# Neighbourhood attention on Trainium2: turned softmax weights in the expansion's PSUM banks, a third row of taps in two halves, and a new order for the second pass

## The chip, the cores and the metric

The kernel runs on one core of a Trainium2 chip. The metric is the device time of one launch in microseconds. Engines are named as in the profile: PE is the matrix engine (TensorE), PEld its weight loads, DVE is VectorE, ACT is ScalarE, POOL is GpSimd, SP is SyncE (it issues the loads and stores). SBUF is the on-chip memory with 128 partitions, PSUM the accumulators of the matrix engine, in banks of 512 float32 per partition.

## The reference

The input `x` is (4, 192, 128, 128) in float32: four images of 192 channels. Two layers follow each other.

Layer 0 is a channel-attention block: a 1x1 convolution to four times 192 channels, a depthwise 3x3 convolution, attention over the 24 channels of each of 8 heads, a gate from pooled values, and a 1x1 projection.

Layer 1 is what the change touches:

```python
pe = depthwise_conv3x3(x, pos_w)
x  = x + pe + pos_b
qkv = einsum('oc,bchw->bohw', qkv_w, x)            # 576 x 192
for i, dil in enumerate((1, 2, 3)):                # 64 channels each, 2 heads of 32
    k, v = 9 reflected neighbours at distance dil of every pixel
    attn = softmax(q . k / sqrt(32))               # over the 9 taps
    out_i = sum over the taps of attn * v
out = einsum('oc,bchw->bohw', proj_w, concat(out_i))
```

So each pixel of each image has 3 dilations x 2 heads x 9 taps of scores.

## The kernel before

The launch has three stages: the first pass (projection and depthwise convolution of layer 0, 0 to about 800 us), the channel attention (to about 1435 us), and the second pass, which applies layer 0's result and computes all of layer 1 (to the end). Only the second pass is changed.

*Tiling.* The second pass works in 64 blocks n. A block is 4 rows of 128 pixels (512 pixels) of a pair of images; blocks 0 to 31 are the first pair. The rows that the neighbours need are kept in rings in SBUF: `hboth` and `hring` for layer 1's input, `kring` and `vring` for keys and values of the three dilations g.

*What a block does*, in the order of its data:
- `loads` (L1089) bring x and v; `h_product` (L1102) makes three tiles of 128 x 512 (two of channels 0 to 127, one for each image, and a third with channels 128 to 191 of both images), and `h_evict` writes them into the rings.
- The position convolution of the first two tiles (`plan_conv`, L1229): `centre` on ACT (L1147) starts a sum in a query bank, `tap` (L1157) adds five taps on DVE, each reading the sum that the one before it wrote; three more taps are multiplied on ACT (`moved`) and added by accumulating transfers that POOL issues. Blocks 0 and 1 do all 8 taps on DVE.
- The third tile's nine taps are multiplied on ACT (`side`, L1192) into three rows of taps, two of these rows are added by accumulating transfers (`side_rows`, L1205), and POOL adds what is left (`side_sum`, L1213).
- `kv_product` (L1269) and `kv_evict` (L1289) fill the key and value rings; `query` and `query_rest` make the queries in PSUM; `prod` (L1346) multiplies on DVE a query with three taps of keys, 128 x 1536 elements; `pick_sums` (L1358) sums the products over the channels into one bank of scores `sc`.
- The softmax is a chain with one step at a time: scores copied by ACT, turned to pixels by PE (`by_pixel`, `st`), maximum and difference on DVE, exponential on ACT, sum on DVE, `divide` on POOL, and then the weights are split into three bf16 parts (`part0`, `rest`, `part1`, `part2`, on ACT and POOL).
- `turn` (L1451) turns the parts back with the rows as partitions, with matmuls of 128 x 128, in three groups i of four, each in a query bank `across`; `turned` (L1456) copies each group by ACT into `e_sb`.
- For each g and each row of taps ty: `expand` (L1495) spreads the weights of three taps over the channels, into the three banks of `ex`; `term` (L1502) multiplies them on DVE with the values, 128 x 1536 elements. The first two rows of taps (ty 0 and 1) are three matmuls on 32 rows each, in different 32-row strips of PE. In the third row, taps 6 and 7 are strips and tap 8 takes rows 0 to 63, because it has no strip of its own.
- `term_sum` (L1513) adds the three terms of a g: the second term is added to the first by an accumulating transfer that POOL issues (where `sent` is true: g = 0 and 1, and all g in the last three blocks) or by POOL; the third by POOL; and POOL then adds the three taps that are left side by side, in two sums of 512.
- `out_product` (L1527) projects, `out_evict` copies by ACT, `store` writes.

*PSUM.* The second pass has four pools: `pc` with two banks (h, k/v and output products), `ex` with one buffer of three banks, `q` with two (queries, the convolution's sums, and `across`), `sc` with one (scores and their turn).

*What sets the order.* Blocks overlap: while block n's weights are expanded, later blocks' products run. The instructions of each engine run in a fixed order, which a planner makes when the program is built. `Schedule` (L37) takes operations with an engine, a cost in microseconds, a rank, what they come after, and for PE the shape of the tile. It plays them engine by engine: of those that are ready it takes the lowest rank, where an operation whose PE shape differs from the last one's has `change_rank` added. It knows a delay of 0.2 between engines and none on the same engine, and 0.1 for a change of shape on PE. The rank is the block number plus an offset from a table, `PLACES` (L344), by `at(name, n, k)` = n + first + step * k. `hold(pool, bufs, first, last)` states that an operation takes a buffer and which operation gives it back, so that buffers limit the overlap. The order that comes out is what the program issues; at run time engines wait for each other by semaphores.

The functions of the second pass that the diff touches are these:

Of the kernel before, what the change touches and what calls it, by code (L numbers as in the profile page):

```python
# [8 lines left out]
BF16 = mybir.dt.bfloat16  # L9
# [10 lines left out]
G = 64  # L20
# [16 lines left out]
class Schedule:  # L37
# [10 lines left out]
    def add(self, engine, rank, cost, run, after=(), shape=None, latency=LATENCY):  # L48
        op = dict(engine=engine, rank=rank, cost=cost, run=run, shape=shape, latency=latency, seq=len(self.ops))
        op.update(after=list(after), first=[], users=[], issued=[])  # L50
        self.ops.append(op)
        return op
# [5 lines left out]
    def order(self):  # L58
# [28 lines left out]
        while events:  # L87
# [5 lines left out]
            for engine, ops in ready.items():  # L93
# [12 lines left out]
                for o in op["users"]:  # L106
                    release(o, end + op["latency"] * (o["engine"] != engine))
# [165 lines left out]
def rows3(t):  # L273
# [11 lines left out]
SUMMED, MOVED, TAP = (0, 1, 2, 7, 5), (3, 8, 6), 0.66  # L285
SLOTS = (0, 2, 4, 6, 1, 3, 5, 7)
# [58 lines left out]
    "loads": (8.8674, 0.08159),  # L345
    "h_product0": (-0.4546, 0.00000),
    "h_evict0": (4.2664, 0.11610),
    "h_product1": (-0.7453, 0.04958),
    "h_evict1": (-5.3389, 0.00000),
    "h_product2": (-0.5800, 0.00000),  # L350
    "h_evict2": (-1.5869, 0.00000),
    "centre": (0.6280, 0.26277),
    "tap": (2.4456, 0.00000),
    "moved": (25.2953, 0.22118),
    "moved_sum0": (8.0617, 0.20067),
    "moved_sum1": (25.2721, 0.04199),
    "side1": (16.4111, 0.19306),
    "side0": (16.3876, 0.02578),
    "side_rows0": (29.3597, 0.01803),
    "side2": (17.3819, 0.22411),  # L360
    "side_rows2": (11.5098, 0.04241),
    "side_sum1": (0.6333, 0.00000),
    "side_sum2": (9.6130, 0.00000),
    "kv0": (1.7001, 0.00000),
    "kvev0": (8.1270, 0.00000),
    "kv1": (2.9139, 0.00000),
    "kvev1": (9.1880, 0.00000),
    "kv2": (2.6117, 0.05333),
    "kvev2": (8.2682, 0.00000),
    "query0": (3.3163, 0.09055),  # L370
    "prod0": (8.3389, 0.00000),
    "query01": (24.1242, 0.00000),
    "term_sent": (10.6067, 0.00000),
    "query1": (3.4334, 0.00000),
    "prod1": (8.6064, 0.00000),
    "query2": (3.6386, 0.11339),
    "prod2": (8.6417, 0.08735),
    "pick0": (-12.0847, 0.00000),
    "pick1": (3.8649, 0.00000),
    "evicted_scores": (-5.2134, 0.00000),  # L380
    "by_pixel": (-11.8436, 0.07637),
    "top": (10.7097, 0.17234),
    "below": (12.3311, 0.00000),
    "exponential": (-3.5826, 0.00000),
    "total": (1.6598, 0.00000),
    "divide": (9.8505, 0.00000),
    "part0": (18.8851, 0.00000),
    "rest": (11.6606, 0.30882),
    "part1": (12.6889, 0.00000),
    "part2": (11.0247, 0.00000),  # L390
# [4 lines left out]
    "term_sum": (13.3772, 0.03133),  # L395
    "out0": (6.5430, 0.07136),
    "outev0": (-1.0619, 0.05980),
    "store0": (8.6802, 0.00000),
    "out1": (6.6681, 3.24309),
    "outev1": (-0.7072, 0.00000),  # L400
    "store1": (0.7313, 0.00000),
# [645 lines left out]
def second_pass(tc, x, w2, xv_p, mix1, mix2, biases, v_dram, v2_dram, out):  # L1047
# [4 lines left out]
    with ExitStack() as ctx:  # L1052
# [12 lines left out]
            (0.1, 3515.2787),  # L1065
# [55 lines left out]
        def plan_h(n):  # L1121
# [5 lines left out]
            for m in range(3):  # L1127
                us, shape = (0.86, FULL) if m < 2 else (0.87, COLS)
# [28 lines left out]
        def tap(n, im, t, last):  # L1157
# [6 lines left out]
            for at, length, o in runs(n, t // 3 - 1, RING, False):  # L1164
# [3 lines left out]
                    posw[:, 0, t : t + 1],  # L1168
                    acc[:, o : o + length],
# [201 lines left out]
        def plan_scores(n, y):  # L1371
            prods, used, picks = [], [], []
            first = [add("PE", at(f"query{g}", n), 0.87, (query, n, g), [y[2]], COLS) for g in range(NG)]
            both = add("PE", at("query01", n), 0.9, (query_rest, n, (0, 1)), first[:2] + y[3], QUARTERS)
# [10 lines left out]
            for row in range(7):  # L1385
                of = prods[4 * row // 3 : min(4 * row + 3, NG * NT - 1) // 3 + 1]
                op = add("PE", at(f"pick{row % 2 * (row < 6)}", n, row // 2), 0.86, (pick_sums, n, row), of, QUADS)
# [63 lines left out]
        def turn(n, i):  # L1451
            across = tile_of("q", ("across", n, i), (128, 4, W))
            for k in range(4):
                mm(across[:, k, :], parts[n % len(parts)][:, 4 * i + k], unit, start=True, stop=True)  # L1454
# [294 lines left out]
```

## Time and profile before

| What | Value |
|---|---|
| median of 3 runs | 4158.29 us (4155.67 to 4160.15) |
| the profiled execution's own time | 4148.03 us |
| its span | 4146.1 us |
| mean granted PE clock | 0.982 |
| busy, share of the span: PE, DVE, ACT, POOL | 97%, 90%, 69%, 75% |
| matmuls | 29088 |

How to read the profile: "busy" is time in which an engine has an instruction in work. Rows of a timeline give the start, the length, the engine, the line of the kernel, the operation, the tile written and the tiles read, the size, and how many instructions the row stands for; what stands in brackets is idle time of the engine before it and which instruction ended it. The length of a row of matmuls reaches to the end of its last result; the next group can start before that, since matmuls overlap, so the distance between the starts of two rows is the better measure of what a group takes. In the page's second part each digit is the busy share of one fortieth of the span, in tenths.

### The profile page before, as it was taken

The page shows a single profiled execution, that of the slowest core. Times are in us where ns is not written, and L with a number is a line of the kernel's source. Part 1 is how long each engine was busy: PE and PEld are TensorE (multiplying, and loading weights), DVE is VectorE, ACT ScalarE, POOL GpSimd, SP SyncE. Part 2 cuts the span into 40 slices and gives each one's busy share as a digit, 9 for nine tenths or more (in the row PEclk, how much of TensorE's full clock was granted, in tenths as well). Part 3 has the DMA queues.
Part 4 walks back from the last instruction along what each step waited for, and adds up shares of the span by engine and source line. Part 5 has one row for each costly group of instructions (what it writes and reads, how often), then busy time and mean ns, then how long its engine had stood idle before and what let it go on. Part 6 is the DMA issues. An engine that isn't in the chain of part 4 may idle for free.

```text
span 4146.1 us, 78135 instructions
## 1 busy us (share of the span) xinstructions
PE 4009.8 (97%) x29088; PEld 1578.6 (38%) x29088; DVE 3737.0 (90%) x4660; ACT 2857.5 (69%) x5337; POOL 3117.8 (75%) x2992
## 2 busy tenths in 40 slices
PE   8999999999999889999999999999999999999996
PEld 3333333356665523333333333333333333333321
DVE  6999999877676569999999999999999999999985
ACT  7999999844454477677676776767677776767741
POOL 6888888745455327888888888888888888888876
PEclk9999999999999999999999999999999999999996
DMA  8888888788778477878788787878878787878734
GB/s 252 267 266 257 270 267 262 227 220 209 199 194 209 124 165 168 185 168 186 169 177 175 171 184 169 181 165 181 174 174 180 170 185 167 186 170 177 154 76 94
DMA packets 404159, 785.08 MB, mean 189 GB/s; under 512 B 48008, under 2 KB 216772, under 8 KB 403780
## 3 DMA queue, kind: packets, MB, share of 16 engines
q0 software_dynamic: 73552, 315.47, 40.2%
q1 hardware_dynamic: 330228, 464.62, 37.5%
q8 instruction: 230, 3.77, 0.4%
q14 instruction: 149, 1.22, 0.1%
HBM read 278.09 MB, written 201.33 MB: 116 GB/s over the span
## 4 chain that ended last, share of the span: by engine, by line
PE 58%; DVE 3%; DMA 2%; issue 1%; POOL 1%; ACT 1%; SPq 0%; POOLq 0%; DVEq 0%; ACTq 0%
PE ph L1110 12%; PE sc L1363 10%; PE pkv L1276 8%; PE ex L1500 5%; PE po L1538 5%; PE pkv L1279 4%; PE q L1333 4%; PE po L1534 4%; PE st L1417 2%; PE q L1344 1%; DVE term L1508 1%; PE q L1340 1%; DVE prod L1352 1%; PE across L1454 1%; DMA side<-side 1%
## 5 line engine op out<-in xcount | busy, mean ns | idle before, releaser
L1352 DVE TENSOR_TENSOR prod<-q,kring 128x1536 f32<-128x1536 f32 (+1 forms) x600 | 997.6, 1685 | 46.0 <-PE sc L1363 32.5
L1508 DVE TENSOR_TENSOR term<-ex,vring 128x1536 f32<-128x1536 f32 (+1 forms) x600 | 1006.7, 1681 | 34.4 <-PE ex L1500 27.7
L1520 POOL TENSOR_TENSOR term<-term,term 128x1536 f32<-128x1536 f32 x253 | 899.4, 3555 | 57.0 <-DMA term<-term 40.9
L592 POOL TENSOR_TENSOR v_True<-v_True,side 128x512 f32<-128x512 f32 (+1 forms) x512 | 643.5, 1268 | 137.8 <-ACT side L581 111.1
L569 DVE SCALAR_TENSOR_TENSOR pa<-vboth,dwv,pa 128x1024 f32<-128x1024 f32 (+1 forms) x448 | 574.2, 1282 | 35.7 <-ACT pa L562 12.2
L1363 PE MATMUL sc<-prod,pick 128*32 128x512 f32 x3456 | 473.1, 603 | 3.1 <-DVE prod L1352 3.1
L1165 DVE SCALAR_TENSOR_TENSOR pa<-hboth,posw,pa 128x512 f32<-128x512 f32 (+1 forms) x524 | 393.0, 750 | 45.8 <-ACT hboth L1114 14.3
L1197 ACT ACTIVATE side<-hring,posw 128x512 f32<-128x512 f32 (+1 forms) x512 | 343.9, 714 | 95.6 <-DMA side<-side 95.5
L1276 PE MATMUL pkv<-y,wkv 128*128 128x512 f32 x768 | 375.4, 610 | 3.4 <-ACT kring L1289 1.4
L515 PE MATMUL pu<-xt,wx 128*128 128x512 f32 x768 | 358.4, 610 | 17.7 <-ACT vboth L551 10.3
L1110 PE MATMUL ph<-lent,mix 128*64 128x512 f32 (+1 forms) x1024 | 368.1, 596 | 4.7 <-DMA mix<-mixed 2.9
L581 ACT ACTIVATE side<-ring,dwv 128x512 f32<-128x512 f32 (+1 forms) x512 | 347.4, 723 | 25.2 <-POOL v_True L592 21.2
L809 DVE BATCH_NORM_STATS2 stats<-conv 128x6 f32<-128x128 f32 x1536 | 303.6, 273 | 61.0 <-ACT conv L807 60.1
L1289 ACT COPY vring<-pkv 64x512 f32<-64x512 f32 x384 | 223.5, 582 | 170.8 <-PE pkv L1279 158.1
L807 ACT COPY conv<-pc 128x512 f32<-128x512 f32 x384 | 228.0, 615 | 157.9 <-PE pc L798 150.1
L1500 PE MATMUL ex<-e_sb,spread 32*128 32x512 bf16 (+1 forms) x1728 | 289.7, 390 | 29.6 <-DVE term L1508 29.6
L798 PE MATMUL pc<-u,band 32*32 32x508 f32 (+1 forms) x6144 | 309.0, 626 | 8.9 <-DMA u<-qk_dram 4.1
L189 POOL COPY band<-few 32x720 f32<-32x720 f32 x180 | 141.6, 787 | 195.6 <-PE pc L798 177.4
L1525 POOL TENSOR_TENSOR acc<-acc,term 128x512 f32<-128x512 f32 x192 | 271.0, 1411 | 8.1
L1522 POOL TENSOR_TENSOR acc<-term 128x512 f32<-128x512 f32 x192 | 265.7, 1384 | 6.7 <-PE po L1534 1.8
L1500 PEld LDWEIGHTS <-spread 32*128 32x128 bf16 (+1 forms) x1728 | 75.1, 91 | 495.4 <-issue 449.4
L1289 ACT COPY kring<-pkv 64x512 f32<-64x512 f32 x384 | 223.2, 581 | 56.2 <-PE pkv L1279 49.1
(189 smaller groups left out, 7075.5 us busy)
## 6 DMA issues: line engine op xcount, KB each, us to landing
term<-term POOLq DMA_DIRECT2D x131, 768.0 KB, 6.5
qk_dram<-us SPq DMA_DIRECT2D x192, 512.0 KB
side<-side POOLq DMA_DIRECT2D x124, 768.0 KB, 8.9
u<-qk_dram SPq DMA_DIRECT2D x512, 128.0 KB
moved<-moved POOLq DMA_DIRECT2D x120, 512.0 KB, 6.0
xt<-in_x SPq DMA_DIRECT2D x64, 512.0 KB
v_dram<-v_False SPq DMA_DIRECT2D x64, 512.0 KB
lent<-in_x SPq DMA_DIRECT2D x128, 256.0 KB
```

What stands on the lines that cost most here:

```text
L515: mm(pu, wx[:, mt * 128 : (mt + 1) * 128], tiles["xt", n][:, im, :], start=True, stop=False)
L569: nc.vector.scalar_tensor_tensor(by_row(to[:, o : o + length]), by_row(vboth[:, at : at + length, :, t % 3 : t % 3 + W]), dwv[:, 0, t : t ...
L592: nc.gpsimd.tensor_add(v[:, rows, :], v[:, rows, :], z[:, rows, :])
L1110: mm(to, w[:, cols], tiles["xv", n, j, im], start=j == 0, stop=j == 2)
L1165: nc.vector.scalar_tensor_tensor(to[:, o : o + length], hboth[:, at : at + length, im, t % 3 : t % 3 + W], posw[:, 0, t : t + 1], acc[:, o ...
L1276: mm(rows3(tile_of("pc", key)), w, tiles["y", n, im], start=True, stop=False)
L1289: nc.scalar.copy(rows[HALVES[im ^ ((kind, g) == ("k", 1))], :, pad : pad + W], rows3(tiles["pkv", n, pair, im])[HALVES[e]])
L1352: nc.vector.tensor_mul(to[:, :, px].rearrange("p t (r w) -> p t r w", w=W), q.unsqueeze(1).to_broadcast([128, 3, *q.shape[1:]]), three,)
L1363: mm(sc[quad * 32 : (quad + 1) * 32, :], pick[:, QR - 4 * row : QR - 4 * row + 32], tiles["prod", n, k // NT, k % NT // 3][:, k % 3, :], s ...
L1500: mm(rows3(ex[:, t % 3, :]), spread[rows, t, :], e_sb[rows], start=True, stop=True)
L1508: nc.vector.tensor_mul(by_row3(to), by_row3(ex), three)
L1520: add_to(first, first, tiles.pop(("term", n, g, k + 1)))
```

## The change

Five things change, all in the second pass.

1. `turn` is one operation of 12 matmuls that writes the three banks of the `ex` pool, and `turned` is one ACT copy of 128 x 1536 elements to bf16. The query banks no longer hold `across`.
2. In `expand`, the third row of taps is done in the order 6, 8, 7, all three as matmuls on 64 rows: taps 6 and 7 on the one half of the rows (`HALVES[1]`), tap 8 on the other. The planner is told the shape ROWS (64 rows) for it.
3. The planner's `add` gets `own`: a delay between an operation and its user on the same engine, 0.13 for the taps. All offsets in `PLACES` are new, so is `change_rank`, and some costs (strips, third row, picks, a query, one h product).
4. In blocks 0 and 1 (`EARLY`) the third tile's position convolution is done as that of the other tiles: a centre on ACT in a query bank and 8 taps on DVE, in place of the nine `side` multiplications, two transfers and two POOL sums.
5. `sent` is true for g = 1 only in odd blocks (before: in all), and nowhere in the last block, n = 63. In the last block the second term is added to the first by DVE, in other cases that aren't sent by POOL.

```diff
-    def add(self, engine, rank, cost, run, after=(), shape=None, latency=LATENCY):
-        op = dict(engine=engine, rank=rank, cost=cost, run=run, shape=shape, latency=latency, seq=len(self.ops))
+    def add(self, engine, rank, cost, run, after=(), shape=None, latency=LATENCY, own=0.0):
+        op = dict(engine=engine, rank=rank, cost=cost, run=run, shape=shape, latency=latency, own=own, seq=len(self.ops))
...
-                    release(o, end + op["latency"] * (o["engine"] != engine))
+                    release(o, end + (op["latency"] if o["engine"] != engine else op["own"]))
...
+EARLY = 2
...
-    "turn": (4.4383, 0.12832),
-    "turned": (9.3688, 0.02210),
-    "expand": (-0.3709, 0.00000),
-    "term": (10.1902, 0.04882),
+    "turn": (-18.1522, 0.07377),
+    "turned": (5.9216, 0.14501),
+    "expand": (-18.0291, 0.00000),
+    "term": (4.9938, 0.00000),
...
-            (0.1, 3515.2787),
+            (0.1, 3164.4328),
...
+        def early_centre(n):
+            at = n * RB % RING
+            nc.scalar.activation(
+                rows3(tile_of("q", ("early", n))),
+                hring[2][:, at : at + RB, 1 : W + 1],
+                AF.Identity,
+                bias=posb[:, 2:3],
+                scale=posw[:, 2, 4:5],
+            )
+
+        def early_tap(n, t, last):
+            acc = to = rows3(tiles["early", n])
+            if last:
+                to = rows3(tile_of("y2", ("y", n, 2)))
+            for at, length, o in runs(n, t // 3 - 1, RING, False):
+                nc.vector.scalar_tensor_tensor(
+                    to[:, o : o + length],
+                    hring[2][:, at : at + length, t % 3 : t % 3 + W],
+                    posw[:, 2, t : t + 1],
+                    acc[:, o : o + length],
+                    ALU.mult,
+                    ALU.add,
+                )
...
-                    prev = add("DVE", at("tap", n, len(summed) * im + j), TAP, (tap, n, im, t, j == len(summed) - 1), [prev])
+                    prev = add("DVE", at("tap", n, len(summed) * im + j), TAP, (tap, n, im, t, j == len(summed) - 1), [prev], own=0.13)
...
+            if n < EARLY:
+                prev = first = add("ACT", at("early_centre", n), 0.65, (early_centre, n), latency=0.3)
+                read("h", 2, n, 0, first)
+                for j, t in enumerate(AROUND):
+                    prev = add("DVE", at("early_tap", n), TAP, (early_tap, n, t, j == 7), [prev], own=0.13)
+                    read("h", 2, n, t // 3 - 1, prev)
+                hold("q", first, prev)
+                return [prev, two, both, [both, prev]]
...
-        def turn(n, i):
-            across = tile_of("q", ("across", n, i), (128, 4, W))
-            for k in range(4):
-                mm(across[:, k, :], parts[n % len(parts)][:, 4 * i + k], unit, start=True, stop=True)
-
-        def turned(n, i):
-            if i == 0:
-                tile_of("e_sb", ("e_sb", n), (128, nh, W), BF16)
-            nc.scalar.copy(tiles["e_sb", n][:, 4 * i : 4 * i + 4, :], tiles.pop(("across", n, i)))
+        def turn(n):
+            across = tile_of("ex", ("across", n), (128, 3, PX)).rearrange("p b (q w) -> p (b q) w", w=W)
+            for k in range(nh):
+                mm(across[:, k, :], parts[n % len(parts)][:, k], unit, start=True, stop=True)
+
+        def turned(n):
+            e_sb = tile_of("e_sb", ("e_sb", n), (128, nh, W), BF16)
+            across = tiles.pop(("across", n))
+            nc.scalar.copy(e_sb.rearrange("p q w -> p (q w)"), across.rearrange("p b w -> p (b w)"))
...
-            out = []
-            for i in range(nh // 4):
-                a = add("PE", at("turn", n, i), 0.3, (turn, n, i), [p2, *out[-1:]], FULL)
-                out.append(add("ACT", at("turned", n, i), 0.58, (turned, n, i), [a, *out[-1:]]))
-                hold("q", a, out[-1])
+            a = then("PE", 0.66, turn, FULL)
+            out = then("ACT", 1.5, turned)
+            hold("ex", a, out)
...
-            for t in range(3 * ty, 3 * ty + 3):
-                rows = slice(0, G) if t == 8 else slice(SLOTS[t] // 2 * STRIP, (SLOTS[t] // 2 + 1) * STRIP)
+            for t in (6, 8, 7) if ty == 2 else range(3 * ty, 3 * ty + 3):
+                strip = SLOTS[t] // 2 * STRIP if t < 8 else 0
+                rows = HALVES[t < 8] if ty == 2 else slice(strip, strip + STRIP)
                 mm(rows3(ex[:, t % 3, :]), spread[rows, t, :], e_sb[rows], start=True, stop=True)
...
-            return ty == 1 and (g < 2 or n >= 2 * NB - 3)
+            return ty == 1 and n < 2 * NB - 1 and (g == 0 or g == 1 and n % 2 or n >= 2 * NB - 3)
...
+                if n == 2 * NB - 1 and k == 0:
+                    add_to = nc.vector.tensor_add
...
-                    ex = add("PE", at("expand", n, k), 0.36 if ty == 2 else 0.25, (expand, n, g, ty), w, STRIPS)
+                    ex = add("PE", at("expand", n, k), 0.43 if ty == 2 else 0.22, (expand, n, g, ty), w, ROWS if ty == 2 else STRIPS)
...
-                            prev = [add("POOL", at("term_sum", n, 4 * g + ty - 1), 3.5, (term_sum, n, g, ty - 1), after)]
+                            engine = "DVE" if n == 2 * NB - 1 and ty == 1 else "POOL"
+                            prev = [add(engine, at("term_sum", n, 4 * g + ty - 1), 3.5, (term_sum, n, g, ty - 1), after)]
```

More of the change, by code (lines that the diff above doesn't have):

```diff
@@ L344 @@
 PLACES = {
[L345 to L388, printed above, removed]
@@ L389 @@
-    "part1": (12.6889, 0.00000),
-    "part2": (11.0247, 0.00000),
-    "turn": (4.4383, 0.12832),
-    "turned": (9.3688, 0.02210),
-    "expand": (-0.3709, 0.00000),
-    "term": (10.1902, 0.04882),
[L395 to L401, printed above, removed]
+    "loads": (0.0099, 0.00000),
+    "h_product0": (-1.1442, 0.03236),
@@ new lines @@
+    "h_evict0": (0.9413, 0.00000),
+    "h_product1": (-0.5417, 0.00000),
+    "h_evict1": (46.0411, 0.00000),
+    "h_product2": (-0.4262, 0.00000),
+    "h_evict2": (-4.6711, 0.09271),
+    "centre": (0.4459, 0.61203),
+    "tap": (0.3422, 0.20258),
+    "moved": (17.0039, 0.14130),
+    "moved_sum0": (1.7081, 0.00000),
+    "moved_sum1": (6.3516, 0.14847),
+    "side1": (-4.7424, 0.01609),
+    "side0": (37.6996, 0.00000),
+    "side_rows0": (5.9045, 0.00000),
+    "side2": (38.3470, 0.27045),
@@ new lines @@
+    "side_rows2": (46.3059, 0.07396),
+    "side_sum1": (34.1352, 0.05190),
+    "side_sum2": (6.6114, 0.00000),
+    "kv0": (2.0359, 0.00000),
+    "kvev0": (4.4411, 0.00000),
+    "kv1": (2.6905, 0.12859),
+    "kvev1": (34.5720, 0.00000),
+    "kv2": (2.8325, 0.02873),
+    "kvev2": (3.1563, 0.00000),
+    "query0": (3.0813, 0.00000),
+    "prod0": (5.9337, 0.00000),
+    "early_centre": (0.8993, 0.00324),
+    "early_tap": (1.4758, 0.00000),
+    "query01": (-36.0721, 0.00000),
+    "term_sent": (-17.9540, 0.18186),
@@ new lines @@
+    "query1": (3.1570, 0.00000),
+    "prod1": (6.2578, 0.00000),
+    "query2": (3.5739, 0.00000),
+    "prod2": (6.7424, 0.00000),
+    "pick0": (-12.7266, 0.06397),
+    "pick1": (4.3024, 0.00000),
+    "evicted_scores": (3.6965, 0.16177),
+    "by_pixel": (-11.9922, 0.00000),
+    "top": (-19.9741, 0.00000),
+    "below": (1.1300, 0.00000),
+    "exponential": (2.8400, 0.11643),
+    "total": (5.4525, 0.00000),
+    "divide": (-10.5681, 0.12415),
+    "part0": (19.3124, 0.00000),
+    "rest": (-5.2533, 0.03124),
@@ L402 @@
+    "part1": (-2.3849, 0.02248),
+    "part2": (5.2677, 0.00000),
+    "turn": (-18.1522, 0.07377),
+    "turned": (5.9216, 0.14501),
+    "expand": (-18.0291, 0.00000),
+    "term": (4.9938, 0.00000),
+    "term_sum": (26.0187, 0.01071),
+    "out0": (6.3347, 0.11390),
+    "outev0": (0.0341, 0.00000),
+    "store0": (25.0600, 0.04627),
+    "out1": (6.6039, 0.21737),
+    "outev1": (1.0223, 0.00000),
+    "store1": (3.5346, 0.12892),
 }
@@ L1127, in plan_h @@
             for m in range(3):
-                us, shape = (0.86, FULL) if m < 2 else (0.87, COLS)
+                us, shape = (0.86, FULL) if m < 2 else (0.86, COLS)
                 ops = [add("PE", at(f"h_product{m}", n, j), us, (h_product, n, m, j), shape=shape) for j in range(3)]
@@ L1373, in plan_scores @@
             first = [add("PE", at(f"query{g}", n), 0.87, (query, n, g), [y[2]], COLS) for g in range(NG)]
-            both = add("PE", at("query01", n), 0.9, (query_rest, n, (0, 1)), first[:2] + y[3], QUARTERS)
+            both = add("PE", at("query01", n), 0.86, (query_rest, n, (0, 1)), first[:2] + y[3], QUARTERS)
             last = add("PE", at("query2", n, 1), 0.86, (query_rest, n, (2,)), first[2:] + y[3], FULL)
@@ L1386, in plan_scores @@
                 of = prods[4 * row // 3 : min(4 * row + 3, NG * NT - 1) // 3 + 1]
-                op = add("PE", at(f"pick{row % 2 * (row < 6)}", n, row // 2), 0.86, (pick_sums, n, row), of, QUADS)
+                op = add("PE", at(f"pick{row % 2 * (row < 6)}", n, row // 2), 0.83, (pick_sums, n, row), of, QUADS)
                 op["after"] += picks[-1:]
@@ L1485, in plan_softmax @@
             stage.schedule.hold("e", len(es), lo, [p2])
-            out = []
-            for i in range(nh // 4):
-                a = add("PE", at("turn", n, i), 0.3, (turn, n, i), [p2, *out[-1:]], FULL)
-                out.append(add("ACT", at("turned", n, i), 0.58, (turned, n, i), [a, *out[-1:]]))
-                hold("q", a, out[-1])
+            a = then("PE", 0.66, turn, FULL)
+            out = then("ACT", 1.5, turned)
+            hold("ex", a, out)
             stage.schedule.hold("parts", len(parts), p0, [a])
-            return out
+            return [out]
         def expand(n, g, ty):
```

## The prediction, made before the changed kernel was run

> **What bounds the kernel now.** I read the page first (engine sums, slices, chain of waits), then a window of the second pass, then single engines in order of time.
>
> ```profile
> span 4146.1 us, 78135 instructions
> ...
> PE 4009.8 (97%) x29088; PEld 1578.6 (38%) x29088; DVE 3737.0 (90%) x4660; ACT 2857.5 (69%) x5337; POOL 3117.8 (75%) x2992
> ...
> PE   8999999999999889999999999999999999999996
> ...
> PE 58%; DVE 3%; DMA 2%; issue 1%; POOL 1%; ACT 1%; SPq 0%; POOLq 0%; DVEq 0%; ACTq 0%
> ```
>
> PE is busy in every slice and carries 58% of the chain that ended last. The stretch that the change touches (from about 1435 us, 64 blocks):
>
> ```profile
> core 0: us, PE busy (x) PEld busy (x) DVE busy (x) ACT busy (x) POOL busy (x), PEclk, DMA share, GB/s
> 2100.00:3700.00 1600.00, 1599.76 (x7484) 553.40 (x7484) 1563.26 (x1290) 1128.33 (x2204) 1333.50 (x952) 1.00 0.81 176
> ```
>
> Here PE has no gap (1599.76 of 1600) at a clock of 1.00, and VectorE is close behind (97.7%); ScalarE (71%) and POOL (83%) have room. So a block costs what its matmul groups cost, start to start. How dense they are:
>
> ```profile
> 2032.31 1.13 PE L1110 MATMUL ph<-lent,wp 128*128 128x512 f32 x2
> 2033.27 1.88 PE L1110 MATMUL ph<-lent,mix 128*128 128x512 f32 x4
> 2034.99 0.39 PE L1454 MATMUL across<-unit,parts 128*128 128x128 bf16 x4
> 2035.31 1.07 PE L1363 MATMUL sc<-prod,pick 128*32 128x512 f32 x8
> 2036.31 0.39 PE L1500 MATMUL ex<-e_sb,spread 32*128 32x512 bf16 x3
> 2036.63 1.98 PE L1276 MATMUL pkv<-y,wkv 128*128 128x512 f32 x4
> ...
> 2046.01 0.71 PE L1500 MATMUL ex<-e_sb,spread 32*128 32x512 bf16 x3
> 2046.65 1.29 PE L1363 MATMUL sc<-prod,pick 128*32 128x512 f32 x8
> ```
>
> The start of the next row minus the start of this one is the price: three strips 0.32, a third row of taps (two strips, then a 64-row matmul) 0.64, four turn matmuls 0.32, or 0.23 when the next group has the same tile shape. Groups behind another shape come out about 0.1 us dearer. Summed so, the program's groups make 40.23 us per steady block; the distance from one block's score turn to the next one's is 40.43. True waits are 0.20 per block: 11.7 us over blocks 3 to 59. From the first `ph` product to the end, 2711 us are 2576 of matmul groups, 37 lost in blocks 0 to 2 (30 before block 0's scores are turned), 12 in steady state, 86 in the last four blocks (51 of them behind block 63's score turn).
>
> **The change, part by part.**
>
> *Matmul work.* Shape changes in the second pass's order fall from 32.2 to 29.8 per block. One turn op of 12 costs 0.73 where three of 4 cost 0.90. The six strip rows and three third rows fall from 3.84 to 3.42, of which the third row is the unsure part. Taps 6 (upper half of the rows) and 8 (lower half) can run together, 0.11 + 0.21; then tap 7 (upper half) needs its weights loaded into rows where tap 6 has just run. If that load lies behind the running matmul the row costs 0.53, if not 0.63. The six `ph` matmuls above take 2.68 from 2032.31 to 2034.99, 0.45 each, though each loads other weights into all rows and the trace gives such a load 0.19: with loads in the open they would need 0.43 + 0.19 = 0.62 each, 3.7 us. The Trainium skill ("TensorE: Matmul & The Clock Gate", Part 3: Packing small matmuls) says the opposite, that a weight load overlaps matmuls in flight only where the row group differs, and so speaks against putting 6 and 7 in one half: by the rule 40.33 us per block, by the row 40.03. I take the row. Other groups lose a little to the new order (output products +0.17, score turn +0.10, scores +0.07, `ph` and queries +0.09): included. All 64 blocks: 2575.7 to 2562.6, **−13.1**.
>
> *The turn in the expansion's banks.* The three-bank expansion buffer exists once. Before, the turned weights lay in the query banks, and 4.5 us of other matmuls stood between the last turn group and the first expansion. Now one turn of 12, one ScalarE copy of 1536 columns and the first expansion follow one another in the same buffer: PE cannot expand until the copy is done. The copy isn't in the trace. From below it is the wider of its relatives, `moved` with 1024 columns, 1.14; from above three copies of 512, 1.75. From 718 ns for 512 and 1144 for 1024 (the two weighted copies) 512 more columns cost 0.43; 0.583 + 2 x 0.43 = 1.44. Last turn matmul 0.22, hand-over 0.04, copy 1.44, hand-over 0.06: 1.76 us from the last turn matmul's start to the expansion. In the new order 28 of 60 blocks have only one group of about 1.06 + 0.15 there; PE waits some 0.55 in 21 of these. In 7 (6, 17, 19, 27, 29, 33, 34) two or three copies of 0.58 out of the k/v banks are queued on ScalarE ahead of it, so 1.0 to 1.6: 11.6 + 8.6 = **+20** (0 if fully covered; 1.0 in each block, +57, if ScalarE is regularly late). Behind the waiting expansion stand the score and k/v products on PE, and then VectorE's products.
>
> *Spacing of taps.* `own` makes the planner put other work between dependent VectorE instructions.
>
> ```profile
> 2053.49 3.12 DVE L1165 SCALAR_TENSOR_TENSOR pa<-hboth,posw,pa 128x512 f32<-128x512 f32 x4
> 2056.65 0.75 DVE L1165 SCALAR_TENSOR_TENSOR y<-hboth,posw,pa 128x512 f32<-128x512 f32 x1
> 2057.31 1.75 DVE L1508 TENSOR_TENSOR term<-ex,vring 128x1536 f32<-128x1536 f32 x1
> ```
>
> The chained y starts 0.04 after the fourth tap's end (2056.61); the independent term starts 0.09 before y's end. The Trainium skill ("VectorE: DVE Perf Modes", Rules for kernel authors) tells to minimise the number of chained operations since the flush of the pipe comes regardless, by which spacing is worth nothing; by the rows each pair taken apart is worth 0.12 us. Neighbours fall from 7 to 2 per steady block, 0.6 us of VectorE. PE's work hides that. It buys only fewer waits of PE for products: the 11.7 us become perhaps 5, **−7** (0 by the rule).
>
> *POOL.* Half the even blocks' share: g = 1 of even blocks is added on POOL (3.56) and not issued as a DMA (0.86), +1.35 per block. POOL goes from 33.7 to 35.0 of 40.4: hidden, and each even block moves one transfer of 768 KB less. If the 5 us of cover were gone it would cost up to 1.35 per block.
>
> *Blocks 0 and 1.* Nine ScalarE copies of 0.72, two transfers and two POOL sums per block are replaced by one ScalarE centre and 8 taps on VectorE: 16 taps x 0.75 = +12 us of VectorE. Before, block 0's products waited for y's last POOL sum, which ended at 1503; VectorE idled in three stretches (13.8, 8.9 and 3.9 us) before 1509. The early taps fill about 4 of these, the spacing saves 3.6 (30 pairs), and the chain over two transfers is gone: **−5** (−9 to +8).
>
> *Last blocks.*
>
> ```profile
> 4122.14 0.86 POOL L1518 DMA_DIRECT2D term<-term  x1 [0.76 <-DVE term L1508]
> ...
> 4127.99 3.42 POOL L1520 TENSOR_TENSOR term<-term,term 128x1536 f32<-128x1536 f32 x1 [2.36 <-DMA term<-term]
> ...
> 4136.93 4.60 PE L1534 MATMUL po<-acc,wo 128*128 128x512 f32 x6 [0.71 <-ACT o L1541]
> ```
>
> In block 63 the second term of every g is issued (0.86) and landed 5.85 us after the issue began, then 3.4 + 1.3 to 1.6 + 1.3 follow on POOL; since the term buffers (two of each kind) hold the next g back, a g costs about 9 us. With an add on VectorE (1.7, as a term of that size) in place of the transfer, POOL's own 6.4 and hand-overs set the step, some 6.7. The last g saves 2.8 outright, the earlier two about as much each: **−8** (±6).
>
> Sum: −13.1 + 20 − 7 − 5 − 8 = −13. The profiled run took 4148.0 (span 4146.1); the median of the runs is 10.3 above it, and I carry the difference over to the median: 4158.3 − 13 = **4145**.
>
> **Rivals.**
> 1. *The turn's copy is covered* (the groups between are longer than counted, or ScalarE is free): the +20 falls away, 4126. For it: 32 of 60 blocks do have more than one group between; ScalarE is 71% busy. Against: in 28 the order is fixed and shorter than the copy. VectorE, 39.0 us busy by the count above, would stand right behind PE's 40.1.
> 2. *The single expansion buffer becomes the bound.* Turn, copy and expansion serialise in each block, and ScalarE, which takes its work in order, brings the copy late in most. At 1.0 us per block it costs 57, +24 net, 4182. It decides above (13 + 20)/60 = 0.55 us per block. For it: before, the turn used two other banks and no term waited for it. Against: 1.76 us is the whole chain, and a group of 1 us always lies in it.
> 3. *The third row's weights can't be loaded behind tap 6* : 0.1 x 3 x 64 = +19, 4164. The `ph` rows speak against it, though they are of another shape and type.
> 4. *It does nothing*: the gain in groups is returned as waits, start and end cancel; 4158. The near-full VectorE speaks for it.
>
> **How the numbers follow.** Forecast 0.40, rival 1 0.16, rival 2 0.24, rival 3 0.12, rival 4 0.08. Below ±0.2% (8.3 us) a measurement of this kernel can't tell a change. Faster: 0.16 + three quarters of the forecast's cases (its own range is 4133 to 4157) = 0.46; same: 0.09 of the forecast, 0.06 of rival 3 and rival 4's 0.06 = 0.21; slower: the rest, 0.33. The range leaves out a tenth on each side: 4120 (rival 1 with a somewhat better end) to 4185 (rival 2).
>
> **What would show it.** Third row: start to next start 0.53 or 0.63. Turn: `ex` after the turn, idle before it put down to ScalarE's `e_sb`, about 20 us in all; its copy 1.44. VectorE: chained neighbours gone, busy per block down 0.6. Window 2100 to 3700: more blocks, PE still near 1600 of 1600 less the waits. Head: block 0's score turn 5 us earlier; tail: the last block's end 8 us closer to its scores. Wrong if `ex` idles over 0.55 us per block, or if the order makes PE wait for q, k or term banks that I have counted as free.

## The result and the profile after

The changed kernel takes 4181.6 us (median of 4 runs, 4180.0 to 4183.7), the kernel before in the same runs 4157.0: a ratio of 1.0067, 95% interval 1.0055 to 1.0080 (brackets behind a ratio hold its interval from here on). It is slower by 0.67%, where 4145 and a gain of 13 us were forecast. The profiled execution has a span of 4178.2 us (4146.1 before) at the same mean clock, 0.982.

The page of the changed kernel, the rows that answer to those of before:

```profile
span 4178.2 us, 78137 instructions
...
PE 3979.5 (95%) x29088; PEld 1564.3 (37%) x29088; DVE 3726.1 (89%) x4679; ACT 2833.6 (68%) x5193; POOL 3189.4 (76%) x2981
...
PE   8999999999999899999999999999999999999995
...
PE 44%; DVE 14%; issue 3%; DMA 2%; POOL 2%; ACT 2%; POOLq 0%; DVEq 0%; SPq 0%; ACTq 0%
```

PE has 30 us less busy time and the span is 32 us longer. The chain that ended last tells more: PE's share fell from 58% to 44%, VectorE's rose from 3% to 14%. Before, the chain of the second pass ran through PE almost alone; now it changes engines. Two windows of the second pass, first of the changed kernel and then of the kernel before, with the busy time of each engine after the window's length:

```profile
1610.00:2850.00 1240.00, 1198.93 (x5631) 403.86 (x5629) 1168.76 (x969) 844.61 (x1601) 1046.37 (x717) 1.00 0.75 162
2990.00:3920.00 930.00, 915.79 (x4349) 316.51 (x4347) 897.66 (x738) 649.90 (x1234) 803.36 (x551) 1.00 0.78 165
```

```profile
1610.00:2850.00 1240.00, 1239.46 (x5795) 427.89 (x5796) 1210.58 (x997) 874.19 (x1705) 1032.33 (x739) 1.00 0.81 176
2990.00:3920.00 930.00, 929.94 (x4355) 320.77 (x4351) 908.67 (x738) 657.85 (x1285) 774.45 (x554) 1.00 0.80 174
```

The clock is 1.00 in all four. In the first window PE's idle time went from 0.5 to 41 us of 1240 and its matmuls from 5795 to 5631; in the second it went from 0.1 to 14 of 930, with as many matmuls as before (4349 and 4355). VectorE is less busy in both. So the early part of the pass lost, with PE and VectorE both idle more, and the late part neither lost nor won.

For a finer division I take the start of each block's score turn (`st`) as a mark, and count from the first `ph` product to the end of the span. Microseconds in one profiled execution of each kernel; the experiments that are told below stand here too:

| kernel | to block 2 | 2 to 14 | 14 to 35 | 35 to 59 | 59 to end | sum |
|---|---|---|---|---|---|---|
| before | 173.9 | 485.7 | 849.4 | 969.8 | 232.2 | 2711.0 |
| after | 169.2 | 511.5 | 866.1 | 968.4 | 223.2 | 2738.5 |
| before, halves alone | 173.9 | 483.1 | 844.6 | 964.6 | 231.0 | 2697.2 |
| before, halves and last block | 172.4 | 483.1 | 844.5 | 965.0 | 231.8 | 2696.8 |
| before, fewer taps | 169.5 | 484.9 | 847.9 | 969.0 | 229.8 | 2701.1 |
| after, strips again | 174.1 | 513.3 | 872.0 | 977.6 | 225.0 | 2762.1 |
| after, no early sums | 188.5 | 510.6 | 848.3 | 968.8 | 225.2 | 2741.5 |
| after, settled order with a seam | 173.2 | 490.2 | 863.1 | 969.7 | 224.5 | 2720.7 |
| the same, short copy | 173.3 | 489.7 | 863.2 | 969.5 | 225.2 | 2721.0 |
| after, settled order | 170.4 | 492.4 | 849.2 | 969.5 | 225.0 | 2706.5 |
| after, fewer taps | 168.6 | 504.7 | 863.4 | 963.2 | 221.5 | 2721.4 |

Between blocks 2 and 35 the changed kernel took 42.5 us more (25.8 + 16.7); the start, the late blocks and the end took 15.1 less. Kernels with the same order up to block 2's mark differ there by some 4 us (169.2, 170.4, 173.2 and 173.3 for the changed kernel and the three made from it by a settled order), so the first column decides nothing at that size.

What PE waited for in the first window, changed kernel (only waits that end in a matmul; us in total, times, longest):

```profile
PE ex L1534 <- DVE term L1542: 11.6, 19, 2.3
PE q L1368 <- DVE prod L1387: 10.1, 15, 1.5
PE ex L1534 <- ACT e_sb L1494: 4.1, 9, 0.5
PE pkv L1311 <- ACT vring L1324: 3.5, 4, 1.5
PE across L1489 <- DVE term L1542: 3.1, 2, 2.0
PE ph L1113 <- ACT vring L1324: 3.0, 5, 0.8
```

The kernel before has two waits there, of 0.4 and 0.2 us. The new ones are for several banks at once: the expansion's (`ex`, `across`), the queries' (`q`), the k/v and h products' (`pkv`, `ph`). The wait for the turned weights, which the prediction put first, is the third row.

What stands behind this is the order. Writing down which groups of matmuls lie between one block's score turn and the next one's, with blocks counted from that turn: in the kernel before the order repeats from block 3 on, mostly every two blocks. In the changed kernel nearly every block up to 35 has an order of its own, and only from 36 on does it repeat. From that my theory was that the loss lies in the unsettled order of blocks 3 to 35 and not in the new operations.

### The profile page after: what moved, and what is told of

Read it like the earlier page. It is cut to its first block, busy times and chain, and to the rows that moved or that the text cites. A ratio compares the mean times of both kernels' runs of the same rounds, so it can differ in the third digit from the quotient of the medians.

```text
span 4178.2 us, 78137 instructions
## 1 busy us (share of the span) xinstructions
PE 3979.5 (95%) x29088; PEld 1564.3 (37%) x29088; DVE 3726.1 (89%) x4679; ACT 2833.6 (68%) x5193; POOL 3189.4 (76%) x2981
## 4 chain that ended last, share of the span: by engine, by line
PE 44%; DVE 14%; issue 3%; DMA 2%; POOL 2%; ACT 2%; POOLq 0%; DVEq 0%; SPq 0%; ACTq 0%
PE ph L1113 9%; PE sc L1398 8%; PE pkv L1311 6%; DVE term L1542 6%; DVE prod L1387 5%; PE q L1368 4%; PE ex L1534 3%; PE pkv L1314 3%; PE po L1570 3%; PE po L1574 2%; DVE pa L1168 2%; PE q L1375 1%; PE q L1379 1%; PE st L1452 1%; DMA term<-term 1%
## 5 line engine op out<-in xcount | busy, mean ns | idle before, releaser
L1556 POOL TENSOR_TENSOR term<-term,term 128x1536 f32<-128x1536 f32 x284 | 1015.1, 3574 | 108.8 <-DMA term<-term 80.3
L1113 PE MATMUL ph<-lent,mix 128*128 128x512 f32 (+1 forms) x1024 | 363.3, 594 | 4.7 <-DMA mix<-mixed 2.4
L1224 ACT ACTIVATE side<-hring,posw 128x512 f32<-128x512 f32 x496 | 335.8, 713 | 29.8 <-DMA side<-side 15.3
L1534 PE MATMUL ex<-e_sb,spread 32*128 32x512 bf16 (+1 forms) x1728 | 273.4, 388 | 56.8 <-DVE term L1542 46.0
L1558 POOL TENSOR_TENSOR acc<-term 128x512 f32<-128x512 f32 x192 | 281.1, 1464 | 12.8 <-PE po L1570 8.1
```

Source lines behind the costliest of these rows:

```text
L1113: mm(to, w[:, cols], tiles["xv", n, j, im], start=j == 0, stop=j == 2)
L1534: mm(rows3(ex[:, t % 3, :]), spread[rows, t, :], e_sb[rows], start=True, stop=True)
L1556: add_to(first, first, tiles.pop(("term", n, g, k + 1)))
```

## The experiments

**The third row in halves, alone and undone.** Both kernels keep the order of their parent on every engine.

```diff
-            for t in range(3 * ty, 3 * ty + 3):
-                rows = slice(0, G) if t == 8 else slice(SLOTS[t] // 2 * STRIP, (SLOTS[t] // 2 + 1) * STRIP)
+            for t in (6, 8, 7) if ty == 2 else range(3 * ty, 3 * ty + 3):
+                strip = SLOTS[t] // 2 * STRIP if t < 8 else 0
+                rows = HALVES[t < 8] if ty == 2 else slice(strip, strip + STRIP)
```

Put into the kernel before:

> The kernel before with the third row of taps in two halves (order 6, 8, 7 on 64 rows each) and nothing else; the planner is not told, so every engine keeps its order. If PE's groups set the end: 0.107 us less in each of 192 third rows, -20 us, about 4137. If VectorE (97.7% busy) takes over at once: its work of about 39.7 us per block leaves room for 0.7 us, so still most of it, but waits of PE for VectorE's terms grow from 13 us to 20 to 30: about 4147. If the weights of tap 7 cannot be loaded behind tap 6 (row 0.63): 0, about 4157.

Measured: 4140.8, ratio to before 0.9973 (0.9963 to 0.9983), about 11 us faster. Taken back in the changed kernel:

> The changed kernel with the third row of taps as it was (two strips and a 64-row matmul), same order on every engine. If PE's groups set the end there too: +20 us, about 4202. If the time is set by waits between PE and VectorE (76 us of idle PE between 1540 and 4090, 24 before), a part of the longer row falls into such waits: +5 to +12, about 4190.

Measured: 4206.7, ratio to before 1.0128 (1.0111 to 1.0145), 25 us slower than the changed kernel, more than either theory had. By the table 4.9 of it lie in the start, where 4 us decide nothing, and 18.7 behind block 2, about what the longer rows add (20). PE's timeline, first of the kernel before with halves and then of the kernel before:

```profile
3322.16 0.60 PE L1501 MATMUL ex<-e_sb,spread 64*128 64x512 bf16 x3
3322.69 1.13 PE L1110 MATMUL ph<-lent,wp 128*128 128x512 f32 x2
```

```profile
3325.35 0.71 PE L1500 MATMUL ex<-e_sb,spread 32*128 32x512 bf16 x3
3325.99 1.12 PE L1110 MATMUL ph<-lent,wp 128*128 128x512 f32 x2
```

From start to next start the row takes 0.53 and 0.64. That is the estimate of the prediction to the hundredth, and the trace's single instructions say why: in a row of this kind tap 7's weight load runs from 0.01 to 0.11 us behind tap 6's start, while tap 6's matmul on the same rows runs to 0.39. So the load lies behind the running matmul, and not after it (0.63). The sentence of the Trainium skill that was weighed ("TensorE: Matmul & The Clock Gate", Part 3: Packing small matmuls) would have it otherwise; the same section also lets a load go ahead that targets a background weight buffer, which would agree. The measured row decides.

Of 0.32 us per block that this takes off PE's groups, 0.22 reached the time between blocks 35 and 59 (969.8 to 964.6 over 24 blocks) in the kernel before. The rest is lost behind one of the three rows: the score sums that follow it start 0.11 earlier, but some of them wait for a product of VectorE that ends as long behind the row's start in both kernels (0.82 us in one block), so that they take 1.22 us in place of 1.12 from start to next start. So VectorE takes a part of the gain.

**The turn alone.** In the first kernel the turn moves into the expansion's banks (`turn` and `turned` as in the change) and nothing else changes, in the second both go back to the query banks and their old form. In both the turn needs another place in the table, first in the one, then in the other:

```diff
-    "turn": (4.4383, 0.12832),
+    "turn": (-0.3710, 0.00000),
```

> The kernel before with only the turn moved: one turn of 12 into the expansion's three banks and one copy of 1536; old table of places, turn ranked just ahead of its first expansion (its old rank would make the buffer's order circular). Theory 'bank' (the single expansion buffer is taken from the terms for about 2.6 us per block and starves VectorE, then PE): +40 to +60 us, about 4200 to 4215, with PE waiting for VectorE's terms and for the copy in each block. Theory 'order' (the new table of places makes the waits, the bank only those for the copy, 10 us): +5 to +20, about 4165 to 4175.

Measured: 4555.3, ratio 1.0972 (1.0950 to 1.0994).

```diff
-    "turn": (-18.1522, 0.07377),
+    "turn": (4.6000, 0.05000),
```

> The changed kernel with only the turn put back: three turns of 4 in the query banks and three copies of 512; new table of places, but the turn ranked n + 4.60 and up (about where the table before has it). Theory 'bank': the waits of PE for terms and for the copy go, about 4130 to 4145. Theory 'order': they stay, less the 10 us of waits for the copy: about 4165 to 4180.

Measured: 4578.6, ratio 1.1016 (1.0991 to 1.1041). Neither theory had said anything like it, and the pair doesn't tell them apart: in both directions one operation of the block gets another form and another place, the planner makes every engine's order anew, and the result is some 400 us worse. Both do worse in the late blocks too (1131 and 1134 us from 35 to 59). Since moving the turn one way and moving it the other both cost that much, its banks alone can't be the reason in both; how much of it the new orders make isn't shown. The first of the two shows one thing more: from about block 8 on its order does repeat, for the most part every three blocks, and a block still takes 46 to 49 us. An order that repeats is not fast for that alone.

**The order alone.** Here all operations stay. Behind block 2's score turn, the operations of the earlier blocks are issued in the order that the planner itself gives to blocks 40 to 51 (12 blocks, after which the rings and the even and odd blocks are back in phase), wherever what they come after allows it.

```diff
+        def place(op):
+            n, i = block(op), index[id(op)]
+            if n >= late:
+                return i
+            m = -((n - src) // period)
+            at = places.get((key(op), n + m * period))
+            return i if at is None else at - m * per
```

First with blocks up to 35 (late = 36, src = 40, period = 12):

> The changed kernel, all operations the same, but behind block 2's score turn the blocks up to 35 take the order, on every engine, that the planner gives to blocks 40 to 51 (its order is a different one in each block up to 35, and repeats from 36 on). Theory 'unsettled order': blocks 3 to 35, which took 42.6 us more than before, fall to the 40.4 us of the late blocks: -35 to -43, about 4139 to 4147. Theory 'bank' or any cause that lies in the operations (the turn in the single expansion buffer, the halves, less sent): no change, about 4180. If the start of the pass is what disturbs the first 33 blocks (something late at run time that is caught up slowly): little change, 4170 to 4180.

Measured: 4163.5, ratio 1.0026 (1.0014 to 1.0038): 18 us better, half of what was expected. The table shows where the other half stayed: blocks 2 to 14 fell from 511.5 to 490.2, but 14 to 35 only from 866.1 to 863.1, and within it the four blocks 31 to 35 took 176.1 us. There the ordered blocks met operations of blocks 36 to 41 that the plan issues ahead of block 36's turn, still at their unsettled places. With late = 42 this seam is gone:

> As the settled order, but with the blocks up to 41 put into the repeated order (the first try left a seam at blocks 31 to 35, where the ordered blocks met the plan's own places for blocks 36 to 41: 176.1 us for four blocks where 161.7 are usual). Theory 'unsettled order': the seam's 14 us go, about 4149; blocks 2 to 59 then take 40.4 us each, as before the change, so nothing is left of the loss and nothing of PE's shorter groups shows either. Otherwise about 4163.

Measured: 4151.9, ratio 0.9991 (0.9979 to 1.0003). The same operations with another order of blocks 3 to 41 are some 30 us faster than the changed kernel (ratios 1.0067 and 0.9991, against the kernel before in each case), and no longer to be told from the kernel before. Up to block 2's score turn the order is the same in both, so the start isn't what slows the blocks behind it. What this shows is that the loss lies in the order of these blocks; it puts a good order in place of bad ones, and so doesn't show that they were bad because they didn't repeat. PE's waits in the same window as above, with the settled order:

```profile
PE ex L1580 <- ACT e_sb L1540: 7.0, 15, 0.5
PE ex L1580 <- DVE term L1588: 5.1, 17, 0.9
PE q L1414 <- DVE y L1213: 3.9, 15, 0.3
PE q L1414 <- DVE prod L1433: 3.9, 19, 0.3
PE ph L1158 <- ACT vring L1370: 0.2, 1, 0.2
```

No wait is longer than 0.9 us, where there were waits up to 2.3; those for k/v banks are all but gone, and the turn's for a term is gone. PE's idle time in this window is 20 us of 1240, half of the changed kernel's 41: what the shorter groups save is spent there.

**Without the early sums.**

```diff
-EARLY = 2
+EARLY = 0
```

> The changed kernel without its early sums (EARLY = 0: blocks 0 and 1 as before), planned anew. The plan then repeats from block 15 on and not from 36. Theory 'unsettled order': 21 blocks less at 1.29 us each, -27, and the start loses the 5 us that the early sums won: about 4155 to 4163. Otherwise the early sums were worth what they were worth: 4181 to 4187.

Measured: 4181.8, ratio 1.0068 (1.0053 to 1.0083): no change in the sum, and by the sum alone this goes against the theory. The segments show two effects that cancel. The order repeats from block 15 on, and 14 to 35 fell from 866.1 to 848.3 (-17.8, where 27 were expected); the start up to block 2 rose from 169.2 to 188.5 (+19.3, where 5 were expected). So the theory holds in its part of the pass. Without the early sums this plan starts 15 us worse than the kernel before (188.5 and 173.9); as the whole plan was made anew, the 19 us are those of the sums and of the order together.

**The short copy.** The settled order (with the seam), and the copy behind the turn cut to a third; two thirds of the turned weights are not copied and stay zero.

```diff
-            nc.scalar.copy(e_sb.rearrange("p q w -> p (q w)"), across.rearrange("p b w -> p (b w)"))
+            nc.scalar.copy(e_sb.rearrange("p q w -> p (q w)")[:, 0:PX], across.rearrange("p b w -> p (b w)")[:, 0:PX])
```

> The kernel with the settled order, and the copy of the turned weights cut from 1536 to 512 columns (the other two thirds of the weights stay zero: they are left out), 0.86 us shorter in every block. If the copy behind the turn in the expansion's only buffer still costs PE time there: its waits for the copy (0.2 us per block in late blocks) go, -10 to -13 against the settled order. If it also starves VectorE of terms: -20 to -25, down to PE's 40.03 us per block. If other work covers it: 0 to -3.

Measured: 4161.2, ratio 1.0021 (1.0013 to 1.0028), against 1.0026 with the full copy; in the profiled executions 2721.0 and 2720.7 us from the first product to the end. The waits of PE between 3200 and 3685 us (12 blocks), first with the full copy and then with the short one:

```profile
PE ex L1580 <- ACT e_sb L1540: 2.8, 6, 0.5
PE q L1414 <- DVE prod L1433: 1.9, 8, 0.6
PE q L1414 <- DVE y L1213: 1.6, 6, 0.3
PE ex L1580 <- DVE term L1588: 1.2, 6, 0.2
```

```profile
PE q L1414 <- DVE prod L1433: 5.2, 8, 1.1
PE q L1414 <- DVE y L1213: 1.6, 6, 0.3
PE ex L1581 <- DVE term L1589: 1.2, 6, 0.2
```

The wait for the copy goes, and what it gave (2.8 us) comes back at the next query, which waits for its bank until VectorE has read it (1.9 to 5.2). In the settled order 0.86 us less of the copy in each block is worth nothing: PE does wait for it, but what comes next would wait without it.

**Less work for VectorE.** From block 2 on taps 0 and 1 are left out in both of the first two tiles, so that the sums lack them; the order is that of the parent.

```diff
+            if 1 < n and t in (0, 1):
+                return
```

In the changed kernel:

> The changed kernel, same order on every engine, but from block 2 on taps 0 and 1 of the first two tiles' position convolution are left out (4 of VectorE's 10 taps, 2.7 to 3.1 us less VectorE per block; the sums lack them). Theory 'hand-overs with VectorE' (PE and VectorE have nearly the same work, and the unsettled order makes them wait for each other): most of the 57 us that PE waits for VectorE go, -40 to -60, about 4122 to 4142. If these waits only stand for a latency elsewhere (softmax chain, POOL, transfers): 0 to -15.

Measured: 4166.3, ratio 1.0029 (1.0017 to 1.0040), 15 us faster. In the kernel before:

> The kernel before with the same 4 taps left out from block 2 on, same order. PE is busy without a gap there, so only its 12 us of waits can go: -3 to -12, about 4141 to 4153. If VectorE was the bound behind PE's full rows (waits inside groups that the rows hide): -20 and more.

Measured: 4148.0, ratio 0.9984 (0.9974 to 0.9994), 6 us faster. The first falls short of what its theory wanted. In blocks 2 to 35, where 42.5 us had been lost, 9.5 came back; 5.2 came back between 35 and 59. So most of what the unsettled blocks lose isn't made by VectorE's load. Even with 3 us less of it per block, VectorE itself waits there, in the window from 1610 to 2850 us of this kernel:

```profile
DVE term L1544 <- PE ex L1536: 73.4, 91, 2.0
DVE prod L1389 <- PE q L1381: 19.6, 21, 3.6
DVE prod L1389 <- PE sc L1400: 18.2, 20, 1.9
```

The engines wait for each other in turn. A piece of the chain that set the end, block 14's, in the changed kernel (start, length, what):

```profile
2103.72 1.11 PE pkv L1314 x4
2104.83 0.56 ACT kring L1324
2105.39 0.01 issue
2105.41 0.59 ACT vring L1324
2106.00 0.04 issue
2106.04 2.84 PE ph L1113 x6
2108.89 0.55 PE ex L1534 x3
...
2109.53 1.77 DVE term L1542
2111.30 0.04 issue
2111.34 0.56 PE ex L1534 x3
```

PE's `ph` stands where its bank is not yet copied out by ScalarE, and two expansions follow each other in PE's order with nothing between them, while the one buffer needs a term of 1.77 us in between.

**The last block.** In the kernel before with halves, the second terms of block 63 are added by VectorE, and nothing is sent there.

```diff
-            return ty == 1 and (g < 2 or n >= 2 * NB - 3)
+            return ty == 1 and n < 2 * NB - 1 and (g < 2 or n >= 2 * NB - 3)
...
+                if n == 2 * NB - 1 and k == 0:
+                    add_to = nc.vector.tensor_add
```

> The kernel before with two parts of the change that leave its order alone: the third row in halves, and in the last block the second terms added by VectorE and not by transfer (nothing sent there). Halves gave -11. The last block's part by its own working -8: together -19, about 4133 to 4139 if the kernel before stands at 4152 to 4158. If the last blocks' gain in the changed kernel (9 us from block 59 to the end) came from its order: -11 only.

Measured: 4142.8, ratio 0.9976 (0.9966 to 0.9987), against 0.9973 with halves alone; from block 59 to the end 231.8 and 231.0 us. The edit is worth nothing. The last g's of this kernel on VectorE, then on POOL:

```profile
4109.01 1.76 DVE L1523 TENSOR_TENSOR term<-term,term 128x1536 f32<-128x1536 f32 x1
...
4113.35 1.76 DVE L1509 TENSOR_TENSOR term<-ex,vring 128x1536 f32<-128x1536 f32 x1 [0.78 <-PE ex L1501]
4115.81 1.76 DVE L1509 TENSOR_TENSOR term<-ex,vring 128x1536 f32<-128x1536 f32 x1 [0.71 <-PE ex L1501]
4117.61 2.78 DVE L1523 TENSOR_TENSOR term<-term,term 128x1536 f32<-128x1536 f32 x1
```

```profile
4112.65 3.43 POOL L1523 TENSOR_TENSOR term<-term,term 128x1536 f32<-128x1536 f32 x1 [5.98 <-DVE term L1509]
...
4117.51 1.26 POOL L1528 TENSOR_TENSOR acc<-acc,term 128x512 f32<-128x512 f32 x1
4122.32 3.42 POOL L1523 TENSOR_TENSOR term<-term,term 128x1536 f32<-128x1536 f32 x1 [3.56 <-DVE term L1509]
```

POOL's sums of two g's start 9.67 us apart (4112.65, 4122.32); with the transfer it was 10.05 (4117.94, 4127.99 before). VectorE now carries the whole g: two terms, the add and the third term, with two hand-overs to PE's expansion between them, and POOL waits for it.

## Why the prediction was wrong

It was wrong in sign: -13 forecast, +25 measured. Step by step:

- *Matmul work, -13.1: nothing speaks against it.* The third row is 0.53. From block 35 on a block took 40.35 us (968.4 / 24), which leaves 0.32 for waits beside the groups' sum of 40.03. The sum itself isn't measured apart from the waits.
- *The steady waits: this is the step that failed.* The prediction wrote that the kernel's 11.7 us "become perhaps 5" and added 20 for the turn's copy, together +13 against what they were. With its own bookkeeping, distance between marks less the groups' sum, blocks 3 to 59 of the changed kernel hold 57 us of waits (2298.4 less 56 x 40.03) where there were 11 (2263.9 less 56 x 40.23): +46. Some 42 of these 46 lie in blocks 3 to 35. PE's idle time in the trace says the same: 57 us over these blocks, where there was 0.3. The working had counted work and looked at single loops in the order (the copy, the expansion buffer), and had taken the other banks as free. It had not looked at whether the order settles at all. Its last sentence named banks "that I have counted as free" as what would make it wrong, without a price; there it went.
- *The turn, +20: mechanism seen, worth over-rated.* The copy takes 1.44 us, as worked out, and PE does wait for it, 23 times and 10.4 us in the whole pass. But taking 0.86 us off each copy changed nothing in the settled order. PE's rows around one turn, then ScalarE's copy:

```profile
2139.35 0.83 PE L1489 MATMUL across<-unit,parts 128*128 128x128 bf16 x12
2140.11 1.13 PE L1314 MATMUL pkv<-y,wkv 64*128 64x512 f32 x4
2141.71 0.39 PE L1534 MATMUL ex<-e_sb,spread 32*128 32x512 bf16 x3 [0.47 <-ACT e_sb L1494]
```

```profile
2140.22 1.44 ACT L1494 CAST e_sb<-across 128x1536 bf16<-128x1536 f32 x1 [4.39 <-PE across L1489]
```

This is the case that the prediction foresaw, one group between turn and expansion and 0.47 us of waiting where it said 0.55.
- *Spacing of taps: right on VectorE, worth nothing.* VectorE's busy time in 2990 to 3920 us fell by 11 us in 23 blocks, 0.48 per block (0.6 were worked out), and no time followed.
- *Start, -5 (-9 to +8): inside its range, but for another reason.* The start differs from before (-4.7) by about as much as it differs between executions. Without the early sums the new plan starts 19 us later, 15 later than the kernel before: the sums seem to save more than was thought, and the new places to cost most of it.
- *Last block, -8 (-14 to -2): wrong.* VectorE's chain sets the step at 9.7 us, not POOL's at 6.7. The changed kernel is 9 us shorter behind block 59's mark, but not by fewer waits: PE is busy 11.8 us less there (179.6 and 167.8) and idle 2.8 more. Of that, its order has done 17 matmuls more (of 754) by the mark, and its groups are shorter.
- *Rivals.* The measured time lies inside the stated range, but by luck: the range's upper end stands on rival 2. Rival 2 (4182) gave the measured time and a wrong cause: it wanted the copy to hold PE in every block, 1.0 us each; that wait is 10.4 us in all, and shortening the copy gained nothing. Whether holding the expansion's banks during the turn costs something in an unsettled order was not separated. Rival 1 (4126; its own terms make 4125) is right that the copy sets little and wrong on what follows, since waits at other banks took its place. Rival 4 is what the settled order shows: the groups' gain is returned as waits, 0.999. Rival 3 falls with the row of 0.53.

What stays open: with the settled order the changed kernel needs 969.5 us for blocks 35 to 59, the kernel before with halves alone 964.6. The rest of the change thus costs some 0.2 us per block even there. Taking some 3 us off VectorE's work in each block of the changed kernel gives as much back (968.4 to 963.2 with fewer taps); which edit brings it, fewer transfers, the turn or the order, no run tells apart, since any of these edits taken back alone makes the planner's order anew. Why the plan doesn't settle before block 36 isn't explained either (it does from about 15 on without the early sums), nor what in the unsettled orders costs the time beyond the waits shown.

The best kernel of these that computes the whole result is the one before with the third row in halves and its own order: 0.9973 of the time before (0.9976 with the last block's edit too).

## What to carry to other kernels

Where a planner writes the order, look at the whole order before costing any single edit: two orders of the same operations are different kernels, and here the difference was 30 us, while the edits that left the order alone were worth 0 to 25. Whether the order repeats from block to block is a quick sign that a plan has settled, but no proof that it is a good one. When two engines are both near full (100% and 97.7%), a sum of busy times says what is possible and not what happens; the waits between them have to be read from the order, bank by bank. An edit that leaves the order alone can be costed from rows: the row came out to the hundredth. The kernel's time followed by 11 of 20 us in one kernel and by 25 in the other, so the waits behind the row have to be read too. Here a table of places that was fitted to one set of operations did not survive another, twice by 400 us.

## What the runs showed of the hardware that was not expected

In these traces an add of two SBUF tiles on VectorE and one on POOL run one after the other, all but some 0.1 us, and not at the same time. VectorE's add of 128x1536 took 1.76 us with POOL idle (4109.01) and 2.78 (4117.61) where POOL's add of 1.26 us had begun 0.1 us ahead (4117.51): POOL's end at 4118.77 and 1.62 more give VectorE's end at 4120.39. In the changed kernel the other order was seen too: a POOL add of this kind, begun 0.17 us behind VectorE's of 1.76 us, took 2.71 in place of 1.26.

```profile
4134.71 1.76 DVE L1556 TENSOR_TENSOR term<-term,term 128x1536 f32<-128x1536 f32 x1
```

```profile
4134.88 2.71 POOL L1561 TENSOR_TENSOR acc<-acc,term 128x512 f32<-128x512 f32 x1
```

All nine kernels here in which VectorE adds two such tiles show the like. The Trainium skill ("VectorE: DVE Perf Modes", Two Vector instructions with no wait between them) mentions a second SBUF read interface that VectorE shares with GpSimd, which agrees. Terms, which read one operand from PSUM, show no such stretch: in the kernel before the 130 that lay beside POOL's sums for nine tenths of their length and more took 1.75 us, the 109 that lay beside none 1.73.

A load of weights for 64 rows was hidden behind a matmul on the same 64 rows (0.53 and not 0.63 us for the row), in both kernels and whether h products, queries, score sums or k/v products came next.
